# The attention of a graph layer by seven half-size products: a transformer-like kernel on one core

## Chip, cores and metric

The kernel runs on one core of a Trainium2 chip. Its time is the device time of one execution in microseconds. A profile of one execution is shown beside the times; its span is that of the profiled execution alone.

## What is computed

The input x holds 64 graphs of 256 nodes with 512 features, all in fp32, and one adjacency matrix `adj` of 256 x 256 that all graphs share. Two layers follow each other, each with a residual and a layer norm:

```python
def layer0(x, adj, Wq, bq, Wk, bk, Wv, bv, Wo, bo):      # 8 heads of 64
    q, k, v = heads(x @ Wq + bq), heads(x @ Wk + bk), heads(x @ Wv + bv)
    scores = einsum('bqhd,bkhd->bhqk', q, k) / 8 + (1 - adj) * -1e9
    return einsum('bhqk,bkhd->bqhd', softmax(scores), v) @ Wo + bo

def layer1(x, W, a, beta, mask):
    h = x @ W
    e = leaky_relu((h @ a1)[:, :, None] + (h @ a2)[:, None, :], 0.2) * mask
    att = softmax(e, axis=2)
    return elu(att @ h + beta * h)

x1 = layernorm(x + layer0(x, adj, ...))
out = layernorm(x1 + layer1(x1, W, a, beta, adj))
```

In the second layer the kernel doesn't form `h` first. It adds beta to the diagonal of `att`, forms y = (att + beta I) x1 in the "spread" stage, as its transpose `yT`, and then u = y W, to which elu is applied.

## The kernel before

Every tensor is laid out in tiles of 128 partitions. A batch is one graph: x1 is a tile `X` of 128 partitions x 2 token blocks x 512 features; transposed tiles such as `xT`, `qT`, `oT` and `yT` have the features on partitions, in four blocks of 128, and the 256 tokens in the free dimension.

**Projections.** `project` multiplies two operands that are each cut into 2 x 2 quarters by Winograd's form of Strassen's method: seven products of half size in place of eight. Some products need sums of quarters as operands. Those of the weights are made once (`weight_sums`), those of a transposed tile for each batch by four chained subtractions on GpSimd (`token_sums`, 128x256 each), one of which overwrites a quarter in place. On TensorE the products run in the order 1, 5, 2, 6, 3, 4, 7 into three PSUM tiles, `chain`, `cross` and `pair`. Product 6 adds onto `chain` after product 1 has been copied out of it, product 3 onto `cross` after product 5, and product 7 onto `chain` after product 6. `gather` gives the two ways out of PSUM: `copy` on ScalarE and `add` on VectorE. For the projection o, both are an addition to `X` on VectorE. A weight quarter has two blocks of 128 along the contraction, so a product that is laid out by feature (q and k) has 2 x 2 matmuls with 128 columns, and one laid out by token (v, o and u) has 2 with 256 columns.

**Spread.** It is the one large product of the second layer that isn't cut in this way. For each of two groups `g`, four matmuls of 256 columns form half of `yT` in a PSUM tile `ps_y`. The first half is copied out by VectorE (L775), the second by ScalarE (L773). Then `token_sums` makes the sums of `yT` for the projection u.

**Order.** All work is entered into a `Plan` as operations with an engine, an assumed duration, reads, writes and buffers. TensorE's order is written out by hand: an operation carries a turn (round, place in `ROUND`), and a round works on several batches at once. In round R it has the mix and o and logits and attention of batch R-1, the scores, sums and v of batch R, x (the transposes), q and k of batch R+1, and spread and u of batch R-2. Of the last 70 TensorE operations the planner may choose the order itself. For the other engines the planner puts operations in the order in which they can start, those with the earliest due time first among equals. Each engine then takes its instructions in that order. Input and output transfers are issued by SyncE.

**Buffers.** Tiles share slots by tag: "x" 5, "full" 9, "half" 24, "xS" 4 (the sums of tokens), "ps" 8 (PSUM banks). A tile takes its slot with its first operation or with the TensorE operation that claims it ahead.

**Names and lines.** L496 transposes x; L499 copies that to xT; L501 adds the output bias to X. L551 is the mix (attention times V), L617 its scaling into oT; L574 the scores; L581, L583 and L585 are mask, exponential and the sum of both key blocks (`both`) on VectorE, ScalarE and GpSimd; L597 the denominators ("sums"); L601 their reciprocal. L360 is any sum of `token_sums`; L382 and L386 are the matmuls of `project` by feature and by token; L517 and L526 its copies and additions, L700 o's additions. L456 to L466 are a layer norm (`rs` on GpSimd in L460 and L461). L715 makes the logits' dot products (`junk`), L725 transposes them (`tr_s`), L735 is the mask of `e` on GpSimd. L753 transposes the attention (`tr_a`), L757 copies it to `attT`, and L768 is the spread.

Of the kernel before, what the change touches and what calls it, by code (L numbers as in the profile page):

```python
# [12 lines left out]
ALU = mybir.AluOpType  # L13
# [3 lines left out]
P = 128  # L17
# [2 lines left out]
ALPHA = 0.2  # L20
NEG = -1000000000.0

ROUND = ("mix", "scores", "x", "spread", "o", "u", "sums", "v", "logits", "q", "k", "attention")
SAFE = 1e15


# [196 lines left out]
def gnn_two_layers(ctx: ExitStack, tc: tile.TileContext, x, adj, Wq, bq, Wk, bk, Wv, bv, Wo, bo, W, a, beta, out):  # L223
    nc = tc.nc
    B, N, D = x.shape
    NT = N // P
    C = D // P
    H = D // HD
    F = D // 2
# [106 lines left out]
    def weight_sums(w, name, engine, reads=()):  # L336

        S = once([3, 2, F], name)
        eng, ns = (nc.vector, 700) if engine == "DVE" else (nc.gpsimd, 1300)
        w11, w12, w21, w22 = ((lambda c=c, i=i: w[:, 2 * c:2 * c + 2, half(i)]) for i in range(2) for c in range(2))  # L340
        s2, s3, s4 = ((lambda i=i: S[:, i]) for i in range(3))

        plan.op(engine, ns, lambda: eng.tensor_tensor(s3(), w11(), w21(), ALU.subtract), [w] + list(reads), [(S, 3)])
        plan.op(engine, ns, lambda: eng.tensor_tensor(w21(), w21(), w22(), ALU.add), [w, (S, 3)], [(S, 1)])
        plan.op(engine, ns, lambda: eng.tensor_tensor(s2(), w21(), w11(), ALU.subtract), [w, (S, 1)], [(S, 2)])
        plan.op(engine, ns, lambda: eng.tensor_tensor(s4(), w12(), s2(), ALU.subtract), [w, (S, 2)], [(S, 4)])

        return [(w11, w), (w12, w), (s4, (S, 4)), (w22, w), (w21, (S, 1)), (s2, (S, 2)), (s3, (S, 3))]

    def token_sums(T, keys, name):  # L350

        S = sb("xS", [3, 2, P], name)
        q = {(k, j): (lambda k=k, j=j: T[:, 2 * k:2 * k + 2, blk(j)]) for k in range(2) for j in range(2)}
        t2, t3, t4 = ((lambda i=i: S[:, i]) for i in range(3))

        def sub(dst, p, m, reads, writes):
            plan.op("POOL", 725, lambda: nc.gpsimd.tensor_tensor(dst(), p(), m(), ALU.subtract), reads, writes)  # L360

        sub(t3, q[1, 1], q[0, 1], [keys(1, 1), keys(0, 1)], [(S, 1)])
        sub(q[0, 1], q[0, 1], q[0, 0], [keys(0, 1), keys(0, 0)], [keys(0, 1)])
        sub(t2, q[1, 1], q[0, 1], [keys(1, 1), keys(0, 1)], [(S, 0)])
        sub(t4, q[1, 0], t2, [keys(1, 0), (S, 0)], [(S, 2)])
        return [(q[0, 0], [keys(0, 0)]), (q[1, 0], [keys(1, 0)]), (q[1, 1], [keys(1, 1)]), (t4, [(S, 2)]),
                (q[0, 1], [keys(0, 1)]), (t2, [(S, 0)]), (t3, [(S, 1)])]

    def project(left, right, by_feature, claims, copy, add):

        shape = [2, P] if by_feature else [F]
        chain, cross, pair = ps(shape, "ps_chain"), ps(shape, "ps_cross"), ps([2] + shape, "ps_pair")

        def product(n, dst, start):
            l, r = left[n - 1][0](), right[n - 1][0]()
            if by_feature:
                for f in range(2):  # L380
                    for c in range(2):
                        nc.tensor.matmul(dst[:, f, :], l[:, c, blk(f)], r[:, c, :],  # L382
                                         start=start and f == 0 and c == 0, stop=c == 1, skip_group_check=True)
            else:
                for c in range(2):
                    nc.tensor.matmul(dst, r[:, c, :], l[:, c, :], start=start and c == 0, stop=c == 1,  # L386
                                     skip_group_check=True)

        def pe(n, buf, part, start, after=()):
            acc = (lambda: buf[A]) if part is None else (lambda: buf[:, part])  # L390
            key = (buf, part)
            plan.op("PE", 895 if by_feature else 870, lambda: product(n, acc(), start), [left[n - 1][1]] + right[n - 1][1] + list(after), [key], claims=claims)
# [58 lines left out]
    left = {}  # L451
# [18 lines left out]
    def batch(b, at, general=False):  # L470

        X = sb("x", [NT, D], f"x_{b}")
        n = b or 0

        def turn(what):

            later = {"x": -1, "q": -1, "k": -1, "scores": 0, "v": 0, "sums": 0, "mix": 1, "o": 1, "logits": 1,
                     "attention": 1, "spread": 2, "u": 2}[what]
            plan.turn = (n + later, ROUND.index(what if b != 0 or what != "sums" else "logits"))

# [3 lines left out]
        def tokens(t):  # L484
            return [(X, (t, 0)), (X, (t, 1))]
# [18 lines left out]
        if b == 0:  # L504
            plan.turn = (0, ROUND.index("spread"))
            left["o"] = residual_bias()
# [3 lines left out]
        right = token_sums(xT, lambda k, j: (xT, j), "xS")  # L510

        def gather(quarter, bias=None):

            def copy(q, acc):
                (dst, key), (src, acc) = quarter(q), acc[::-1]
                if bias is None:
                    plan.op("ACT", 400, lambda: nc.scalar.copy(dst(), src()), [acc], [key])  # L517
# [229 lines left out]
        tra = ps([NT, N], "tr_a")  # L747
        attT = sb("half", [NT, N], "attT")
# [5 lines left out]

        turn("attention")
        plan.op("PE", 430, pe_att, [e], [tra], claims=[attT])
        plan.op("ACT", 590, lambda: nc.scalar.copy(attT[A], tra[A]), [tra], [attT])  # L757

        yT = sb("full", [C, N], f"yT_{b}")

        def spread(g):
            acc = ps([2, N], "ps_y")

            def pe():
                for i in range(2):
                    c = 2 * g + i
                    for j in range(NT):
                        nc.tensor.matmul(acc[:, i, :], X[:, j, c * P:(c + 1) * P], attT[:, j, :],  # L768
                                         start=j == 0, stop=j == NT - 1)

            plan.op("PE", 1720, pe, tokens(0) + tokens(1) + [attT], [acc], claims=[yT])
            if g:
                plan.op("ACT", 590, lambda: nc.scalar.copy(yT[:, 2 * g:2 * g + 2, :], acc[A]), [acc], [(yT, g)])  # L773
            else:
                plan.op("DVE", 690, lambda: nc.vector.tensor_copy(yT[:, 2 * g:2 * g + 2, :], acc[A]), [acc], [(yT, g)])  # L775

        turn("spread")
        for g in range(2):
            spread(g)
        right_y = token_sums(yT, lambda k, j: (yT, k), "yS")  # L780
        u = sb("full", [NT, D], f"u_{b}")
        turn("u")
        project(left["w"], right_y, False, [u], *gather(
# [3 lines left out]
        for t in range(NT):  # L787
            m = sb("half", [D], "m")
# [12 lines left out]
    for b in range(B):  # L801
        batch(b, slice(b, b + 1))
# [6 lines left out]
    def check():  # L809
# [5 lines left out]
            claims=[least])  # L815
# [9 lines left out]
    with tc.If(again != 0):  # L825
# [40 lines left out]
```

## Time and profile before

| | |
|---|---|
| median of three runs | 2891.65 us (2891.22 to 2893.65) |
| span of the profiled execution | 2892.0 us |
| granted TensorE clock, mean | 0.995 |
| matmuls of the spread (L768) | 1024 records, 236.0 us |
| GpSimd, mean of one L360 | 725 to 738 ns at 128x256 |
| bytes moved by DMA | 110.89 MB, 38 GB/s |

In the profile PE is TensorE's matmul side, PEld its weight loads, DVE VectorE, ACT ScalarE, POOL GpSimd and SP SyncE. An fp32 matmul of the program appears as two records, and the recorded durations of successive matmuls overlap; the cost of a stage is read from the distance between starts. Lines of groups give the operation, out<-in and shapes, how many, busy time, mean duration, and the idle time before them with what ended it. Lines in order of time give start, duration, engine, line and operation, and in brackets the idle time before and its releaser.

### The profile page before, as it was taken

The numbers are of one execution on the slowest core, as the hardware profiler recorded it, in microseconds if no ns is written. First come the engines' busy times: TensorE is split into PE (matmuls) and PEld (weight loads), VectorE is DVE, ScalarE is ACT, GpSimd is POOL, SyncE is SP. The second block draws the span as 40 slices with busy tenths as digits, with TensorE's granted clock in tenths as the row PEclk, the third lists the DMA queues.
The fourth block names the chain that finished last, engine by engine and source line by source line (L and its number), as shares of the span: only waits on it lengthen the run. The fifth ranks groups of instructions, "written<-read, shape, count | busy, mean of one in ns | idle before, by whom it ended". The sixth has DMA issues, their size and how long they took to land.

```text
span 2892.0 us, 51909 instructions
## 1 busy us (share of the span) xinstructions
PE 2852.6 (99%) x19605; PEld 2477.5 (86%) x19605; DVE 1895.8 (66%) x4322; ACT 1293.3 (45%) x3201; POOL 1361.9 (47%) x2010
## 2 busy tenths in 40 slices
PE   8999999999999999999999999999999999999996
PEld 7888888888888888888888888888888888888884
DVE  5666666666666666666666666666666666666666
ACT  3444444444444444444444444444444444444442
POOL 6454453553544544535535445445355354454543
PEclk9999999999999999999999999999999999999998
DMA  3001011011011010111110110111101101111000
GB/s 132 24 30 45 30 38 45 30 38 44 25 44 38 30 45 30 38 45 30 37 45 23 45 37 31 45 30 37 45 30 38 45 23 45 35 33 45 30 23 31
DMA packets 75407, 110.89 MB, mean 38 GB/s; under 512 B 5904, under 2 KB 39440, under 8 KB 75152
## 3 DMA queue, kind: packets, MB, share of 16 engines
q1 hardware_dynamic: 75024, 107.50, 11.3%
q8 instruction: 158, 2.59, 0.4%
q14 instruction: 97, 0.79, 0.1%
q0 software_dynamic: 128, 0.01, 0.0%
HBM read 73.41 MB, written 34.08 MB: 37 GB/s over the span
## 4 chain that ended last, share of the span: by engine, by line
PE 97%; DVE 1%; POOL 1%; issue 0%; DMA 0%; ACT 0%; POOLq 0%; DVEq 0%
PE ps_chain L386 17%; PE ps_chain L382 12%; PE ps_pair L386 11%; PE ps_cross L386 11%; PE ps_cross L382 8%; PE ps_pair L382 8%; PE ps_sc L574 8%; PE ps_pv L551 8%; PE ps_y L768 8%; PE tr_x L496 2%; PE ps_den L597 2%; PE tr_a L753 1%; PE tr_s L725 0%; DVE junk L715 0%; DMA beta_sb<-in_L_gnn_beta_dram 0%
## 5 line engine op out<-in xcount | busy, mean ns | idle before, releaser
L360 POOL TENSOR_TENSOR oS<-oT 128x256 f32<-128x256 f32 x128 | 93.7, 732 | 725.1 <-DVE oT L617 720.0
L583 ACT ACTIVATE pT<-pT 128x512 f32<-128x512 f32 x512 | 297.7, 627 | 303.2 <-DVE pT L581 303.2
L735 POOL TENSOR_TENSOR e<-e,adj_sb 128x512 f32<-128x512 f32 x64 | 81.6, 1275 | 662.4 <-DVE e L733 656.4
L585 POOL TENSOR_TENSOR both<-pT 128x256 f32<-128x256 f32 x512 | 360.9, 734 | 35.8 <-ACT pT L583 35.8
L581 DVE TENSOR_TENSOR pT<-ps_sc,maskT_sb 128x512 f32<-128x512 f32 x512 | 317.4, 682 | 22.8 <-PE ps_sc L574 22.7
L517 ACT COPY u<-ps_chain 128x256 f32<-128x256 f32 x128 | 47.6, 372 | 442.6 <-PE ps_chain L386 442.6
L574 PE MATMUL ps_sc<-qT,kT 64*128 64x256 f32 x2048 | 238.4, 382 | 0.0
L768 PE MATMUL ps_y<-attT,x 128*128 128x256 f32 x1024 | 236.0, 384 | 1.4 <-ACT attT L757 1.4
L551 PE MATMUL ps_pv<-pT,v 128*64 128x256 f32 x2048 | 235.1, 382 | 0.0
L574 PEld LDWEIGHTS ps_sc<-qT,kT 64*128 64x128 f32 x2048 | 192.8, 187 | 43.8 <-issue 24.0
L768 PEld LDWEIGHTS ps_y<-attT,x 128*128 128x128 f32 x1024 | 192.0, 193 | 26.7 <-ACT attT L757 2.2
L551 PEld LDWEIGHTS ps_pv<-pT,v 128*64 128x64 f32 x2048 | 141.4, 137 | 75.5 <-issue 10.3
L466 ACT ACTIVATE x<-x,nmr,rs 128x512 f32<-128x512 f32 x256 | 194.5, 809 | 17.4 <-DVE nmr L464 17.4
L617 DVE TENSOR_TENSOR oT<-ps_pv,inv_all 128x512 f32<-128x512 f32 x128 | 88.5, 692 | 162.2 <-PE ps_pv L551 162.2
L700 DVE TENSOR_TENSOR x<-x,ps_chain 128x256 f32<-128x256 f32 x256 | 102.1, 420 | 138.0 <-PE ps_chain L386 137.2
L715 DVE SCALAR_TENSOR_TENSOR junk<-x,wa_sb 128x512 f32<-128x512 f32 x256 | 165.3, 701 | 0.9 <-ACT x L466 0.9
L501 POOL TENSOR_TENSOR x<-x,res_sb 128x512 f32<-128x512 f32 x128 | 164.4, 1285 | 3.1 <-DVE res_sb L422 3.1
L456 DVE BATCH_NORM_STATS2 bn<-x 128x6 f32<-128x512 f32 x256 | 164.1, 683 | 2.2
L520 ACT ACTIVATE qT<-ps_chain,bq_sb 128x128 f32<-128x128 f32 x256 | 80.3, 365 | 187.9 <-PE ps_chain L382 187.9
L461 POOL TENSOR_TENSOR rs<-rs,neg_half 128x1 f32<-128x1 f32 x256 | 144.2, 563 | 21.3
L382 PE MATMUL ps_chain<-xS,sq_sb 128*128 128x128 f32 x1024 | 135.9, 276 | 0.0
L382 PE MATMUL ps_chain<-xS,sk_sb 128*128 128x128 f32 x1024 | 135.4, 275 | 0.0
(174 smaller groups left out, 6799.0 us busy)
## 6 DMA issues: line engine op xcount, KB each, us to landing
x<-in_x_dram SPq DMA_DIRECT2D x64, 512.0 KB, 3.7
inv_all<-rows SPq DMA_DIRECT2D x128, 256.0 KB, 3.6
out_dram<-x SPq DMA_DIRECT2D x128, 256.0 KB, 2.0
wq_sb<-in_L_gnn_Wq_dram SPq DMA_DIRECT2D x1, 1024.0 KB
wk_sb<-in_L_gnn_Wk_dram SPq DMA_DIRECT2D x1, 1024.0 KB
wo_sb<-in_L_gnn_Wo_dram SPq DMA_DIRECT2D x1, 1024.0 KB
wv_sb<-in_L_gnn_Wv_dram SPq DMA_DIRECT2D x1, 1024.0 KB
w_sb<-in_L_gnn_W_dram SPq DMA_DIRECT2D x1, 1024.0 KB, 14.4
```

What stands on the lines that cost most here:

```text
L382: nc.tensor.matmul(dst[:, f, :], l[:, c, blk(f)], r[:, c, :], start=start and f == 0 and c == 0, stop=c == 1, skip_group_check=True)
L386: nc.tensor.matmul(dst, r[:, c, :], l[:, c, :], start=start and c == 0, stop=c == 1, skip_group_check=True)
L456: plan.op("DVE", 690, lambda: nc.vector.bn_stats(bn[A], X[:, t, :]), [(X, (t, 0)), (X, (t, 1))], [bn])
L466: plan.op("ACT", 810, lambda: nc.scalar.activation(X[:, t, :], X[:, t, :], AF.Identity, bias=nm[A], scale=rs[A]), [nm, rs], [(X, (t, 0)), ...
L501: plan.op("POOL", 1270, lambda: nc.gpsimd.tensor_tensor(X[:, t, :], X[:, t, :], res_sb[A], ALU.add), [res_sb], tokens(t))
L551: nc.tensor.matmul(acc[s * HD:(s + 1) * HD, i, :], V[:, k, h * HD:(h + 1) * HD], pT[h][:, k, :], start=k == 0, stop=k == NT - 1)
L574: nc.tensor.matmul(acc[i + s][:, k, :], kT[r:r + HD, h // 2, blk(k)], qT[r:r + HD, h // 2, :], start=True, stop=True)
L581: plan.op("DVE", 690, lambda h=h, i=i: nc.vector.tensor_add(pT[h][A], acc[i][A], maskT_sb[A]), [acc[i], maskT_sb], [pT[h]])
L583: plan.op("ACT", 620, lambda h=h: nc.scalar.activation(pT[h][A], pT[h][A], AF.Exp, scale=1.0 / HD ** 0.5), [pT[h]], [pT[h]])
L585: plan.op("POOL", 725, lambda h=h: nc.gpsimd.tensor_tensor(both[h // 2][:, h % 2, :], pT[h][:, 0, :], pT[h][:, 1, :], ALU.add), [pT[h]], [ ...
L715: plan.op("DVE", 780, lambda t=t, i=i, junk=junk: nc.vector.scalar_tensor_tensor(junk[A], X[:, t, :], 1.0, wa_sb[:, i, :], op0=ALU.mult, o ...
L768: nc.tensor.matmul(acc[:, i, :], X[:, j, c * P:(c + 1) * P], attT[:, j, :], start=j == 0, stop=j == NT - 1)
```

## The change

The spread is computed by `project` as well. Its left operands are the four quarters of x1 (token block by half of the features) and four sums of them (128x256 each, in a new "full" tile `X_sums`); its right operands are the four 128x128 quarters of the transposed attention, one of them overwritten in place, and three sums (in a new "xS" tile). All eight sums are made on GpSimd. A quarter has one block along the contraction (`inner=1`), so that a product has two matmuls with 128 columns. The four quarters of `yT` come out of PSUM by `gather`: four copies on ScalarE and four additions on VectorE. The two `ps_y` tiles and their two copies are gone. `project` takes a list of dependencies for a left operand too.

In `ROUND`, o follows scores and the spread follows o; x comes after the spread, where it was ahead of it; u moves from behind o to behind the logits, ahead of q.

```diff
-ROUND = ("mix", "scores", "x", "spread", "o", "u", "sums", "v", "logits", "q", "k", "attention")
+ROUND = ("mix", "scores", "o", "spread", "x", "sums", "v", "logits", "u", "q", "k", "attention")
...
-    def project(left, right, by_feature, claims, copy, add):
+    def project(left, right, by_feature, claims, copy, add, inner=2):
...
-                    for c in range(2):
+                    for c in range(inner):
                         nc.tensor.matmul(dst[:, f, :], l[:, c, blk(f)], r[:, c, :],
-                                         start=start and f == 0 and c == 0, stop=c == 1, skip_group_check=True)
+                                         start=start and f == 0 and c == 0, stop=c == inner - 1,
+                                         skip_group_check=True)
...
-        plan.op("ACT", 590, lambda: nc.scalar.copy(attT[A], tra[A]), [tra], [attT])
+        plan.op("ACT", 590, lambda: nc.scalar.copy(attT[A], tra[A]), [tra], [(attT, i) for i in range(4)])
+
         yT = sb("full", [C, N], f"yT_{b}")
-
-        def spread(g):
-            acc = ps([2, N], "ps_y")
-
-            def pe():
-                for i in range(2):
-                    c = 2 * g + i
-                    for j in range(NT):
-                        nc.tensor.matmul(acc[:, i, :], X[:, j, c * P:(c + 1) * P], attT[:, j, :],
-                                         start=j == 0, stop=j == NT - 1)
-
-            plan.op("PE", 1720, pe, tokens(0) + tokens(1) + [attT], [acc], claims=[yT])
-            if g:
-                plan.op("ACT", 590, lambda: nc.scalar.copy(yT[:, 2 * g:2 * g + 2, :], acc[A]), [acc], [(yT, g)])
-            else:
-                plan.op("DVE", 690, lambda: nc.vector.tensor_copy(yT[:, 2 * g:2 * g + 2, :], acc[A]), [acc], [(yT, g)])
-
+        S, T = sb("full", [4, F], "X_sums"), sb("xS", [3, P], "att_sums")
+        x1 = {(i, c): (lambda i=i, c=c: X[:, c, half(i)]) for i in range(2) for c in range(2)}
+        aq = {(c, j): (lambda c=c, j=j: attT[:, c, blk(j)]) for c in range(2) for j in range(2)}
...
+        pool(725, sums[2], x1[0, 0], x1[1, 0], sub, tokens(0), [(S, 3)])
+        pool(725, sums[0], x1[1, 0], x1[1, 1], add, tokens(0) + tokens(1), [(S, 1)])
+        pool(725, sums[1], sums[0], x1[0, 0], sub, tokens(0) + [(S, 1)], [(S, 2)])
+        pool(725, sums[3], x1[0, 1], sums[1], sub, tokens(1) + [(S, 2)], [(S, 4)])
+        pool(450, tsum[1], aq[1, 1], aq[0, 1], sub, [attT], [(T, 1)])
+        pool(450, aq[0, 1], aq[0, 1], aq[0, 0], sub, [(attT, 0), (attT, 1), (attT, 2), (attT, 3), (T, 1)], [(attT, 1)])
+        pool(450, tsum[0], aq[1, 1], aq[0, 1], sub, [(attT, 3), (attT, 1)], [(T, 0)])
+        pool(450, tsum[2], aq[1, 0], tsum[0], sub, [(attT, 2), (T, 0)], [(T, 2)])
...
         turn("spread")
-        for g in range(2):
-            spread(g)
-        right_y = token_sums(yT, lambda k, j: (yT, k), "yS")
+        project(left_x, right_a, True, [yT], *gather(
+            lambda q: (lambda: yT[:, 2 * q[0]:2 * q[0] + 2, blk(q[1])], (yT, q))), inner=1)
+        right_y = token_sums(yT, lambda k, j: (yT, (k, j)), "yS")
```

More of the change, by code (lines that the diff above doesn't have):

```diff
@@ L346, in weight_sums @@
         plan.op(engine, ns, lambda: eng.tensor_tensor(s4(), w12(), s2(), ALU.subtract), [w, (S, 2)], [(S, 4)])
-        return [(w11, w), (w12, w), (s4, (S, 4)), (w22, w), (w21, (S, 1)), (s2, (S, 2)), (s3, (S, 3))]
+        return [(w11, [w]), (w12, [w]), (s4, [(S, 4)]), (w22, [w]), (w21, [(S, 1)]), (s2, [(S, 2)]), (s3, [(S, 3)])]
     def token_sums(T, keys, name):
@@ L391, in pe @@
             key = (buf, part)
-            plan.op("PE", 895 if by_feature else 870, lambda: product(n, acc(), start), [left[n - 1][1]] + right[n - 1][1] + list(after), [key], claims=claims)
+            plan.op("PE", 448 * inner if by_feature else 870, lambda: product(n, acc(), start),
+                    left[n - 1][1] + right[n - 1][1] + list(after), [key], claims=claims)
             return key, acc
@@ new lines, in batch, with pool @@
+        x1 = {(i, c): (lambda i=i, c=c: X[:, c, half(i)]) for i in range(2) for c in range(2)}
+        aq = {(c, j): (lambda c=c, j=j: attT[:, c, blk(j)]) for c in range(2) for j in range(2)}
+        sums = [(lambda i=i: S[:, i]) for i in range(4)]
+        tsum = [(lambda i=i: T[:, i]) for i in range(3)]
+        def pool(ns, dst, p, m, op, reads, writes):
+            plan.op("POOL", ns, lambda: nc.gpsimd.tensor_tensor(dst(), p(), m(), op), reads, writes)
+        sub, add = ALU.subtract, ALU.add
@@ new lines, in batch, with one @@
+        pool(450, tsum[0], aq[1, 1], aq[0, 1], sub, [(attT, 3), (attT, 1)], [(T, 0)])
+        pool(450, tsum[2], aq[1, 0], tsum[0], sub, [(attT, 2), (T, 0)], [(T, 2)])
+        def one(ap):
+            return lambda: ap().unsqueeze(1)
+        s1, s2, s3, s4 = ((one(sums[k]), [(S, k + 1)]) for k in (0, 1, 2, 3))
+        left_x = [(one(x1[0, 0]), tokens(0)), (one(x1[0, 1]), tokens(1)), s4, (one(x1[1, 1]), tokens(1)), s1, s2, s3]
+        right_a = [(one(aq[0, 0]), [(attT, 0)]), (one(aq[1, 0]), [(attT, 2)]), (one(aq[1, 1]), [(attT, 3)]),
+                   (one(tsum[2]), [(T, 2)]), (one(aq[0, 1]), [(attT, 1)]), (one(tsum[0]), [(T, 0)]),
+                   (one(tsum[1]), [(T, 1)])]
```

## The prediction

> **What bounds the kernel now.** I read the page's busy times first, then the busy time by stretch, then the order of time on TensorE, then the groups, and last the other engines' order of time.
>
> ```profile
> PE 2852.6 (99%) x19605; PEld 2477.5 (86%) x19605; DVE 1895.8 (66%) x4322; ACT 1293.3 (45%) x3201; POOL 1361.9 (47%) x2010
> ```
>
> A busy share proves little by itself, as matmul records overlap. The busy time of one round (the columns are PE, PEld, DVE, ACT, POOL, then the granted clock) says more:
>
> ```profile
> 1426.53:1470.76 44.23, 44.23 (x307) 38.52 (x307) 29.24 (x68) 20.15 (x50) 20.91 (x31) 1.00 0.11 37
> ```
>
> PE is never without a matmul at full clock; no other engine is busy over two thirds of the round. 64 rounds of 44.23 us are 2830.7 us of the 2892.0 us span; the other 61 us are head and tail. So a round costs what TensorE must issue, plus any wait that grows past its slack. In order of time on PE (start, us, what):
>
> ```profile
> 1414.39 1.06 PE L382 MATMUL ps_cross<-xT,wq_sb 128*128 128x128 f32 x8
> 1415.28 1.06 PE L382 MATMUL ps_pair<-xT,wq_sb 128*128 128x128 f32 x8
> ...
> 1426.53 3.67 PE L551 MATMUL ps_pv<-pT,v 128*64 128x256 f32 x32
> 1430.14 3.72 PE L574 MATMUL ps_sc<-qT,kT 64*128 64x256 f32 x32
> 1433.79 1.09 PE L496 MATMUL tr_x<-ident,x 128*128 128x128 f32 x8
> 1434.72 3.62 PE L768 MATMUL ps_y<-attT,x 128*128 128x256 f32 x16
> 1438.18 1.03 PE L386 MATMUL ps_chain<-wo_sb,oT 128*128 128x256 f32 x4
> ...
> 1444.22 1.03 PE L386 MATMUL ps_chain<-w_sb,yT 128*128 128x256 f32 x4
> 1445.08 1.03 PE L386 MATMUL ps_cross<-w_sb,yT 128*128 128x256 f32 x4
> ```
>
> Costs are distances of starts. Every written matmul is two records. The spread takes 1438.18 - 1434.72 = 3.46 us for 16 records, 216 ns each at 256 columns. A product of the q projection takes 0.893 us for 8, 112 ns each at 128 columns. Halving the columns halves the cost, weight loads included.
>
> The rest I need is how fast ACT answers PE, and what POOL does:
>
> ```profile
> 1445.34 0.37 ACT L517 COPY u<-ps_chain 128x256 f32<-128x256 f32 x1 [5.85 <-PE ps_chain L386]
> ```
>
> ```profile
> 1431.03 0.72 POOL L360 TENSOR_TENSOR oS<-oT 128x256 f32<-128x256 f32 x1 [11.65 <-DVE oT L617]
> 1431.83 0.73 POOL L360 TENSOR_TENSOR oT<-oT 128x256 f32<-128x256 f32 x1
> ```
>
> ```profile
> 2866.80 0.59 ACT L757 COPY attT<-tr_a 128x512 f32<-128x512 f32 x1 [2.61 <-PE tr_a L753]
> ...
> 2867.43 5.34 PEld L768 LDWEIGHTS ps_y<-attT,x 128*128 128x128 f32 x16 [1.08 <-ACT attT L757]
> ```
>
> A copy starts 0.26 us after its product's last issue slot (1445.08 to 1445.34), takes 0.37 us, and PE goes on 0.04 us after ACT ends (2867.39 to 2867.43). POOL's dependent sums follow each other every 0.81 us, and POOL stands idle 11.65 us before oS in every round.
>
> [...] the trace has 0.893/4 = 223 ns per written matmul. [...] (8 loads hide in each 0.893 us). [...] four L715 operations beside POOL took up to 1.74 us instead of 0.69.
>
> **The change part by part.**
>
> *Spread on PE.* Removed: 8 matmuls of 256 columns, 3.46 us. Added: 7 products of 2 matmuls of 128 columns, 28 records x 111.65 ns = 3.126 us. Gain 0.334 us a round, 64 x 0.334 = 21.4 us. Loads rise from 16 to 28, but in the q ratio of one load to 112 ns, where they are hidden.
>
> *Copies out of PSUM.* ACT loses one 0.586 us copy and gets four of 0.37: +0.9, 21.0 us a round. DVE loses 0.69 and gets four adds of 0.42: +1.0, 30.2 us. Neither fills 43.9 us. But `chain` and `cross` are reused inside the project, and its products are now 0.447 us long. Product 6 may write `chain` only after the copy that follows product 1. Two products, 0.893 us, lie between; the loop is 0.26 + 0.37 + 0.04 = 0.67. Slack 0.22 us, or 0.11 if the load, one 0.11 us slot ahead, must also keep its place. The same holds for 5 to 3 and 6 to 7. If ACT is free, it costs nothing; bound 0 to 0.11 us each.
>
> *Sums on POOL.* Four of 128x256 at 0.81: 3.2 us. The 128x128 size is in no row; 732 and 1275 ns at 256 and 512 elements give 0.46 us, with the 0.08 us step 0.54; at worst as dear as 256, 0.81. Four are 2.2 us (to 3.2). POOL rises from 20.9 to 26.3 of 43.9 us. The attention sums start when attT lands, 0.76 us after the mix begins, and end by 3.0; oS queues behind them and is ready only at 4.5. The spread needs them from 13.8. The sums of x1 have from about 19 us of one round to 13.3 of the next. Hidden, by the projections' matmuls.
>
> *The order.* From the old durations, with 0 at the mix: scores 3.6, o 7.3, spread 13.3, x 16.4, sums 17.4, v 18.5, logits 24.6, u 24.8, q 30.8, k 37.0, attention 43.3, end 43.9. What now comes due earlier:
> - o at 7.3 instead of 11.65. Its product 1 waits for POOL's second sum (it overwrites a part of oT), ready at 4.5 + 2 x 0.81 = 6.1. Slack 1.2. DVE must put o's adds before some pT adds; the first has 1.7 us to be done in, against 0.26 + 0.42 + 0.04 and one pT add of 0.68.
> - sums at 17.4 instead of 23.8. POOL ends oS at 7.7, then eight `both` at 0.70: 13.3. Slack 4. Even one x + res (1.29) in between fits.
> - logits at 24.6. From the end of o (1444.22) to the end of the last junk (1453.33) is 9.1 us now; 13.3 + 9.1 = 22.4. Slack 2.2.
> - u at 24.8: yT is added up by 17.5, yS takes 3.2 us, x + res and rs 4.1: done by 24.8; its first POOL result is needed at 25.6. The end of logits to attention grows from 12.7 to 18.7 us, so nothing there.
> The x load on SP moves 9 us later with its transposes, 13 us ahead of q. The output DMAs follow u and go 7 us later; nothing but the x slots waits for them.
>
> *Buffers.* "full" gets a ninth tile per batch for nine slots. X_sums lives about 40 us; at the worst I count xT, qT, kT, V, inv_all, oT or u, X_sums and yT partly overlapping, seven or eight. xS peaks at three of four. PSUM: o's first bank is the first score bank, free at 5.4.
>
> *Head and tail.* PE waited 4.3 us before the first tr_s; x now lies between o and it, so up to 0.9 less. In the tail the last spread waits for POOL's 2.2 us beside its first two products: about 1 us more. The free reordering window of 70 PE entries covers fewer rounds. I take 0, bounds -3 and +4 us.
>
> Sum: -21.4 + 0 against the 2892.0 us span. The three runs lie at 2891.22 to 2893.65 around 2891.65, from which I subtract: 2870.3.
>
> **The rivals.**
>
> *A: ACT's queue stops the short spread.* ACT takes its instructions in the order that the planner wrote; an exponential of 627 ns (L583) or a norm's 809 ns (L466) in front of the copy of `chain` makes PE late by 0.627 - 0.11 = 0.52 or 0.70 us. It decides from 0.334 us a round: one such meeting a round makes it slower, by 64 x (0.52 - 0.334) = 12 to 64 x 0.37 = 23 us: 2903 to 2915. For it: the last exponential ends 13.0 us after the mix now, and the spread begins at 13.3. Against it: the pT adds of DVE lose the yT copy from their midst, ACT loses two xT copies there, and norm x1 follows o's end by 5.6 us, after the spread. But o's adds now lie among the pT adds.
>
> *B: small stalls eat part of it.* POOL at `both` or yS, DVE at o's adds, or the tight copy loop at 0.1 us each: 0.1 to 0.25 us a round, 2876.7 to 2886.
>
> *C: it isn't less work for PE.* If 28 loads bound at their recorded 192 ns, the spread would take 5.4 us and the kernel 124 us more. The q products exclude it.
>
> **How the numbers follow.** A measurement of this kernel can tell about 0.2%, 5.8 us, from no change. No new wait, 2866 to 2875: 0.63. B with a visible gain: 0.14. Gains and stalls within 0.2% of each other: 0.08. Slower, A with what is left of C: 0.15. So faster 0.77, same 0.08, slower 0.15. The range takes the first case with the end bounds, and B: 2864 to 2889.
>
> **What would show it.** Right: rounds of 43.89 us, PE gapless; the spread 3.13 us from its first product to tr_x; POOL near 26 us a round. The chain copies in the spread start 0.26 us after their product. Wrong: idle PE or PEld in front of a spread product put down to ACT's yT (A), or in front of o, ps_den, tr_s or u (B); or a spread over 3.3 us with no wait.

## The result and the profile after

The changed kernel takes 2875.74 us, the median of four runs (2874.54 to 2876.21); the kernel before takes 2892.19 us, the median of four (2891.22 to 2893.65). The ratio is 0.9942, with an interval of 0.9925 to 0.9959: 16.5 us faster. The forecast was 21.4 us faster. The two profiled spans are 2892.0 and 2874.1 us, 17.9 us apart.

The busy times of the page:

```profile
PE 2838.8 (99%) x20373; PEld 2489.0 (87%) x20373; DVE 2072.5 (72%) x4514; ACT 1385.9 (48%) x3393; POOL 1757.7 (61%) x2522
```

One steady round (the columns are PE, PEld, DVE, ACT, POOL, granted clock, DMA share, GB/s):

```profile
1415.28:1459.35 44.07, 44.07 (x319) 38.71 (x318) 32.11 (x71) 21.63 (x53) 27.10 (x39) 1.00 0.11 37
```

A round lasts 44.07 us where it lasted 44.23 and 43.89 was forecast. POOL carries about what was forecast (26.3), DVE 1.9 us more than its 30.2, and PE is still the engine without a gap. The round, in order of time on PE (start, us):

```profile
1418.89 3.72 PE L576 MATMUL ps_sc<-qT,kT 64*128 64x256 f32 x32
1422.54 1.13 PE L387 MATMUL ps_chain<-wo_sb,oT 128*128 128x256 f32 x4
1423.51 1.03 PE L387 MATMUL ps_cross<-wo_sb,oT 128*128 128x256 f32 x4
...
1428.69 0.61 PE L382 MATMUL ps_chain<-attT,x 128*128 128x128 f32 x4
1429.13 0.61 PE L382 MATMUL ps_cross<-attT,X_sums 128*128 128x128 f32 x4
1429.58 0.61 PE L382 MATMUL ps_pair<-attT,x 128*128 128x128 f32 x4
1430.03 0.61 PE L382 MATMUL ps_chain<-att_sums,X_sums 128*128 128x128 f32 x4
...
1431.81 1.04 PE L498 MATMUL tr_x<-ident,x 128*128 128x128 f32 x8
1432.78 1.07 PE L599 MATMUL ps_den<-both,ones 128*32 128x256 f32 x16
...
1439.93 0.51 PE L727 MATMUL tr_s<-ident,s 128*128 128x128 f32 x2
1440.27 1.03 PE L387 MATMUL ps_chain<-w_sb,yT 128*128 128x256 f32 x4
```

The spread takes 1431.81 - 1428.69 = 3.12 us, a product every 0.445 to 0.45 us with no stall. But the two `tr_s` take 0.34 us up to u's first product, where they took 0.22, and o's first product takes 0.97 where its next takes 0.86. The weight loads show why `tr_s` is late:

```profile
1439.71 0.14 PEld L727 LDWEIGHTS tr_s<-ident,s 128*128 128x128 f32 x1
1440.11 0.13 PEld L727 LDWEIGHTS tr_s<-ident,s 128*128 128x128 f32 x1 [0.26 <-DVE junk L717]
```

The second of them waits for the last logit product on DVE. The view of waits has this for the whole kernel (total us, times, longest us); it counts the idle time of the weight loads, of which PE loses 0.12 us a round:

```profile
PEld tr_s L727 <- DVE junk L717: 22.9, 65, 2.5
```

Before, the same wait came four times. What DVE does up to that product in the kernel before (the last of the four logit products, then the reciprocal), and what POOL did last:

```profile
1452.64 0.69 DVE L715 SCALAR_TENSOR_TENSOR junk<-x,wa_sb 128x512 f32<-128x512 f32 x1
...
1453.25 1.75 DVE L601 RECIPROCAL inv<-ps_den 128x256 f32<-128x256 f32 x1
```

```profile
1460.67 1.28 POOL L735 TENSOR_TENSOR e<-e,adj_sb 128x512 f32<-128x512 f32 x1 [10.64 <-DVE e L733]
```

There POOL stands idle for 10.64 us, beside all four products. DVE in the kernel after:

```profile
1433.94 1.76 DVE L603 RECIPROCAL inv<-ps_den 128x256 f32<-128x256 f32 x1 [0.18 <-PE ps_den L599]
1435.62 1.03 DVE L717 SCALAR_TENSOR_TENSOR junk<-x,wa_sb 128x512 f32<-128x512 f32 x1
...
1438.84 1.21 DVE L717 SCALAR_TENSOR_TENSOR junk<-x,wa_sb 128x512 f32<-128x512 f32 x1
1439.98 0.08 DVE L717 DVE_READ_ACCUMULATOR junk<-x,wa_sb 128x1 f32 x1
```

and POOL at the same time:

```profile
1437.31 1.05 POOL L360 TENSOR_TENSOR xT<-xT 128x256 f32<-128x256 f32 x1
...
1439.58 1.06 POOL L360 TENSOR_TENSOR xS<-xT,xS 128x256 f32<-128x256 f32 x1
```

The reciprocal now stands ahead of the logit products; before it stood behind them. And the products share their time with POOL's sums of `xT`: they take up to 1.21 us instead of 0.69, the sums 1.06 instead of 0.73; these are DVE's 1.9 us. The last product ends at 1440.06, 11.37 us after the end of o (1428.69), where it was 9.1 us before.

Where the 17.9 us of span come from: the second mix starts at 93.42 us instead of 99.81, which is 6.4 us (both read from the chain of work that ended last, which puts a mix 0.07 us later than the order of time does). The 60 rounds from there bring 60 x 0.16 = 9.7. The rest, the tail above all, is 138.6 us before and 136.8 after: 1.8.

### The profile page after: what moved, and what is told of

It reads as the page before. It is cut to its first block, busy times and chain, and to the rows that moved or that the text cites. A ratio compares the mean times of both kernels' runs of the same rounds, so it can differ in the third digit from the quotient of the medians.

```text
span 2874.1 us, 54166 instructions
## 1 busy us (share of the span) xinstructions
PE 2838.8 (99%) x20373; PEld 2489.0 (87%) x20373; DVE 2072.5 (72%) x4514; ACT 1385.9 (48%) x3393; POOL 1757.7 (61%) x2522
## 4 chain that ended last, share of the span: by engine, by line
PE 98%; DVE 1%; POOL 0%; issue 0%; DMA 0%; ACT 0%; POOLq 0%; DVEq 0%
PE ps_chain L387 18%; PE ps_chain L382 15%; PE ps_pair L387 11%; PE ps_cross L387 11%; PE ps_cross L382 10%; PE ps_pair L382 10%; PE ps_sc L576 8%; PE ps_pv L553 8%; PE ps_den L599 2%; PE tr_x L498 2%; PE tr_a L755 1%; PE tr_s L727 1%; DVE junk L717 0%; DMA beta_sb<-in_L_gnn_beta_dram 0%; PE ps_b L420 0%
## 5 line engine op out<-in xcount | busy, mean ns | idle before, releaser
L585 ACT ACTIVATE pT<-pT 128x512 f32<-128x512 f32 x512 | 312.1, 630 | 448.0 <-DVE pT L583 444.3
L462 POOL TENSOR_SCALAR rs<-mv 128x1 f32<-128x1 f32 x256 | 55.9, 219 | 504.3 <-DVE mv L459 504.3
L717 DVE SCALAR_TENSOR_TENSOR junk<-x,wa_sb 128x512 f32<-128x512 f32 x256 | 282.3, 1154 | 0.4 <-ACT x L468 0.3
L770 POOL TENSOR_TENSOR att_sums<-attT 128x128 f32<-128x128 f32 x128 | 58.8, 459 | 323.6 <-ACT attT L759 318.6
L468 ACT ACTIVATE x<-x,nmr,rs 128x512 f32<-128x512 f32 x256 | 200.7, 808 | 72.1 <-DVE nmr L466 63.6
L463 POOL TENSOR_TENSOR rs<-rs,neg_half 128x1 f32<-128x1 f32 x256 | 144.7, 565 | 21.4
L360 POOL TENSOR_TENSOR xS<-xT 128x256 f32<-128x256 f32 x128 | 140.8, 1100 | 8.1 <-ACT xT L501 3.1
L387 PE MATMUL ps_chain<-so_sb,oS 128*128 128x256 f32 x512 | 131.5, 379 | 0.0
L387 PE MATMUL ps_chain<-sw_sb,yS 128*128 128x256 f32 x512 | 131.5, 379 | 0.0
```

The source lines that it names most:

```text
L468: plan.op("ACT", 810, lambda: nc.scalar.activation(X[:, t, :], X[:, t, :], AF.Identity, bias=nm[A], scale=rs[A]), [nm, rs], [(X, (t, 0)), ...
L585: plan.op("ACT", 620, lambda h=h: nc.scalar.activation(pT[h][A], pT[h][A], AF.Exp, scale=1.0 / HD ** 0.5), [pT[h]], [pT[h]])
L717: plan.op("DVE", 780, lambda t=t, i=i, junk=junk: nc.vector.scalar_tensor_tensor(junk[A], X[:, t, :], 1.0, wa_sb[:, i, :], op0=ALU.mult, o ...
```

## The experiments

The theory at first: the products bring their 0.33 us a round, and the new order takes half of it back at its seams and at `tr_s`; the 6.4 us of the head belong to the order as well. The rival: the shorter spread itself is what stalls, or it makes the next stages late. Each experiment changes one thing. This table has the stages of one steady round on PE as distances of starts, in us, for those that differ (mix 3.60, scores 3.65, sums 1.00, q and k 6.25 each and attention 0.53 are the same in all):

| kernel | round | x | o | spread | v | logits | u | second mix starts |
|---|---|---|---|---|---|---|---|---|
| before | 44.23 | 0.93 | 6.04 | 3.46 | 6.15 | 0.22 | 6.14 | 99.81 |
| after | 44.07 | 0.97 | 6.15 | 3.12 | 6.15 | 0.34 | 6.05 | 93.42 |
| order only | 44.27 | 0.97 | 6.15 | 3.45 | 6.15 | 0.22 | 6.05 | 93.59 |
| products only | 43.92 | 0.93 | 6.05 | 3.15 | 6.15 | 0.22 | 6.14 | 98.14 |
| logits behind u | 44.16 | 0.96 | 6.15 | 3.19 | 6.30 | 0.22 | 6.04 | 92.17 |
| x ahead of o | 44.77 | 0.93 | 6.36 | 3.22 | 6.15 | 0.78 | 6.05 | 97.70 |
| new order in round 1 alone | 43.92 | as products only | | | | | | 93.41 |
| reciprocal behind the junks | 43.94 | 0.97 | 6.15 | 3.12 | 6.15 | 0.22 | 6.05 | 93.54 |
| GpSimd held | 43.95 | 0.97 | 6.15 | 3.12 | 6.15 | 0.22 | 6.05 | 92.25 |

**The order alone.** The kernel before with the new `ROUND`, and nothing else:

```diff
-ROUND = ("mix", "scores", "x", "spread", "o", "u", "sums", "v", "logits", "q", "k", "attention")
+ROUND = ("mix", "scores", "o", "spread", "x", "sums", "v", "logits", "u", "q", "k", "attention")
```

> The kernel before with the new order of a round alone; the spread stays one product of 256 columns. Theory 1 (boundaries): the round pays for the order what the changed kernel shows against 44.23 us: +0.11 us where o instead of x follows the scores, +0.04 for the transposes ahead of the denominators, -0.09 for u no longer ahead of them; 44.29 us if the logits don't wait, 44.41 if they do. Theory 2: the order is free and it is the short products that cost 0.18 us a round more than worked out: 44.23 us here. Of the head, theory 1 says that the 6.4 us gained up to the second mix come from the order (o and its norm start earlier): the second mix starts near 93.5 us; if they come from the products, near 99.8. Total by theory 1: -3 to +5 us against the kernel before.

It took 2890.75 us, the kernel before in the same runs 2892.72; the ratio is 0.9993 (0.9985 to 1.0002), not told from no change. Its head has the whole gain (second mix at 93.59) and its rounds lose 0.04 us each: o costs 0.10 more behind the scores, x 0.04 more ahead of the sums, u 0.09 less. `tr_s` doesn't wait: the last junk ends at 1446.54, 11.44 us after the end of o, and `tr_s` comes at 1446.67. It is just met. So the path to the logits is as long here as in the kernel after; the longer spread hides it.

**The products alone.** The kernel after with the old `ROUND`.

```diff
-ROUND = ("mix", "scores", "o", "spread", "x", "sums", "v", "logits", "u", "q", "k", "attention")
+ROUND = ("mix", "scores", "x", "spread", "o", "u", "sums", "v", "logits", "q", "k", "attention")
```

> The changed kernel with the old order of a round. Theory 1: the products bring their whole 0.334 us: rounds of 43.89 us, the second mix near 99.8 us as before, 2871 to 2873 us in all, so 3 to 5 us less than the changed kernel. Theory 2 (short products cost more than worked out, or need the other order since u comes 6 us after the spread): rounds of 44.0 us or more with idle PE in front of a spread product or of u, 2878 us or more.

2873.29 us, ratio 0.9933 (0.992 to 0.9947). The rounds are 0.31 us shorter, and the head gains 1.7 us only. The logit products are stretched here too: beside the new sums of x1 on POOL three of the four take 1.20 us, and the last ends 11.22 us after o, where it was 9.1. In this order that is still 2.06 us ahead of `tr_s`. Here, with the spread close behind the exponentials, ScalarE does what rival A feared. In order of time:

```profile
1425.61 0.63 ACT L585 ACTIVATE pT<-pT 128x512 f32<-128x512 f32 x1
1426.23 0.37 ACT L519 COPY yT<-ps_chain 128x256 f32<-128x256 f32 x1
1426.50 0.64 ACT L585 ACTIVATE pT<-pT 128x512 f32<-128x512 f32 x1
```

and PE beside it:

```profile
1426.03 0.61 PE L382 MATMUL ps_cross<-attT,X_sums 128*128 128x128 f32 x4
1426.48 0.63 PE L382 MATMUL ps_pair<-att_sums,x 128*128 128x128 f32 x4
1426.95 0.61 PE L382 MATMUL ps_chain<-att_sums,X_sums 128*128 128x128 f32 x4
```

Exponentials lie between the copies, yet only one distance is longer, 0.47 instead of 0.45. The copy of product 6 starts 0.20 us after its product's last issue slot (1426.03), as early as a free ScalarE would start it, since the exponential ahead of it ends just then; it is done at 1426.60, 0.35 us ahead of product 7. The exponentials are where rival A puts them, and the spread is 0.02 us longer than in the kernel after. The longer distance is that of product 4, which writes the second half of `pair`: its weight load waits for DVE's addition out of the first half, which ended at 1426.28, and starts at 1426.40, 0.03 us later than the others' distance would have it.

**Logits behind u.** If the wait of `tr_s` is the loss, a later place takes it away:

```diff
+ROUND = ("mix", "scores", "o", "spread", "x", "sums", "v", "u", "logits", "q", "k", "attention")
```

> The changed kernel with u ahead of the logits. Theory 1: the second tr_s transpose waits 0.12 us a round for the last dot product of the logits, which GpSimd's sums beside it stretch from 0.69 to 1.20 us; with 6 us more there is no wait, and the round is 43.95 us, 7 us less in all: 2868 to 2870 us. The dot products stay near 1.2 us. Rival: the attention now gets its inputs too late (logits to attention are back at 12.7 us, with more work on DVE and GpSimd), tr_a waits, and the round is 44.07 us or more.

2878.37 us, ratio 0.9953 (0.9939 to 0.9967): this expectation was missed. `tr_s` is back at 0.22, but v now takes 6.30 us. ScalarE, in order of time:

```profile
1437.41 0.39 ACT L606 ACTIVATE junk<-ps_den 128x256 f32<-128x256 f32 x1 [1.44 <-DVE inv L603]
...
1437.78 0.36 ACT L519 COPY v<-ps_chain 128x256 f32<-128x256 f32 x1
```

The activation of L606 reads the PSUM tile that the reciprocal on DVE also reads, and waits until that is done. v's copy stands behind it in ScalarE's queue, v's next product on `chain` waits for the copy: products at 1437.28, 1438.20 and 1439.17, distances of 0.92 and 0.97 instead of 0.86. The spread took 0.06 more: its sixth product, product 4 again, came 0.06 us late behind an addition of `yT` on DVE (ended 1432.44, load of the product at 1432.49). That is read from one trace and wasn't tested.

**x ahead of o.** Only x's place goes back, and u behind the logits stays; x is then no seam behind the spread:

```diff
+ROUND = ("mix", "scores", "x", "o", "spread", "sums", "v", "logits", "u", "q", "k", "attention")
```

> The changed kernel with x right behind the scores again (logits still ahead of u). Theory 1: the first product after the scores pays for its first weight load: o's start costs 0.11 us, that of the transposes 0.04; GpSimd can make the sums of xT earlier, so the dot products of the logits meet less of it and tr_s falls from 0.34 to 0.22 us: 43.87 to 43.95 us a round, 2864 to 2869 us. Rival (tr_s at 0.34 us is the price of going from a transpose to a product of 256 columns, not a wait): tr_s stays at 0.34 and the round is near 44.0 us, 2871 us. Second rival: x and its sums of xT crowd out the sums for the spread or both, and PE waits: over 44.07 us.

2923.19 us, ratio 1.0105 (1.0089 to 1.012): 30 us slower, where a gain was expected. The wait of `tr_s` grows to 0.78 - 0.22 = 0.56 us, as x no longer lies between o and the logits. o is 0.31 us longer: in a steady round the load of its product 4 starts at 1408.86, as DVE's addition out of the first half of `pair` ended only at 1408.74, behind two mask additions (1.28 us). That is one of the places of rival B, o's adds; it is read from the trace and wasn't tested. The spread's 0.1 us lies in its last distance, ahead of the sums (0.54 instead of 0.445), where u pays the same in the old order. That the wait grows when the time from the end of o to the logits shrinks fits the theory; the late product and the seam were left out of the expectation. The head has little of its gain (97.7), as x is ahead of o in the first round too.

**The new order in round 1 alone.** If the head's 6.4 us come from the order of the first round, they can be had without the 0.15 us that the order costs in each later one:

```diff
-            plan.turn = (n + later, ROUND.index(what if b != 0 or what != "sums" else "logits"))
+            order = EARLY if n + later == 1 else ROUND
+            plan.turn = (n + later, order.index(what if b != 0 or what != "sums" else "logits"))
```

`EARLY` is the new order and `ROUND` the old one.

> The seven products with the old order of a round, but in round 1 alone the new order (o right behind the scores, x after it). Theory: the head of the kernel gains 4.7 us on the products with the old order (second mix at 93.4 instead of 98.1 us), as o of the first batch starts earlier and the first tr_s no longer leaves TensorE idle so long that its clock drops; the rounds stay at 43.92 us: 2873.3 - 4.7 = 2868.6 us. Rival: the time is only moved (round 2 or the tail gives it back): 2873 us.

2867.19 us against 2892.03 of before: ratio 0.9914 (0.9901 to 0.9928), below both kernels. The rounds are those of the products alone, the second mix starts at 93.41. What happens in the head, in the kernel before:

```profile
83.70 0.48 PE L725 MATMUL tr_s<-ident,s 128*128 128x128 f32 x1 [1.96 <-DVE junk L715]
83.97 1.92 PE L382 MATMUL ps_chain<-xT,wq_sb 128*128 128x128 f32 x8
85.68 1.91 PE L382 MATMUL ps_cross<-xT,wq_sb 128*128 128x128 f32 x8
```

and after:

```profile
80.15 0.32 PE L727 MATMUL tr_s<-ident,s 128*128 128x128 f32 x1 [1.52 <-DVE junk L717]
80.31 1.06 PE L382 MATMUL ps_chain<-xT,wq_sb 128*128 128x128 f32 x8
81.20 1.06 PE L382 MATMUL ps_cross<-xT,wq_sb 128*128 128x128 f32 x8
```

The logits are ready 3.55 us sooner (80.15 for 83.70). With x behind it and fewer late products, o ends at 70.25 instead of 71.79 (1.54 us); the first junk starts 5.70 us after that instead of 6.27 (0.57); and the four junks take 4.15 us instead of 5.59 (1.44), as POOL's operations of 512 elements, x + res and a sum of the weights, beside which three of them took 1.62 to 1.74, are elsewhere (three take 1.20 now, beside sums of 256 columns). The q products then start every 0.89 us instead of every 1.71, at a granted clock of 1.00 from the start of q to the mix. The busy time by stretch of the kernel before has 0.50 in its clock column after the wait:

```profile
83.90:89.00 5.10, 5.10 (x25) 5.10 (x25) 1.89 (x5) 1.25 (x4) 1.27 (x1) 0.50 0.00 0
```

From the start of q to the mix it is 15.77 us before and 13.04 after, 2.73 less. Together with 3.55, and 0.11 less at `tr_s`, that is the 6.4. The slow products stand behind the longer idle times: 2.32 + 1.96 = 4.28 us of idle PE before, with one short transpose between, were followed by 5.1 us at 0.50; behind the 1.5 us after, and the 2.06 us in the kernel with the order alone, the products start every 0.89 us from the first on. With the products alone, behind 1.76 + 1.94 = 3.70 us, the first three q products take 1.34, 1.71 and 1.26 us and the next ones 0.89, so that q to the mix takes 14.67 us there; 1.1 of the 1.7 us that its head gains are this. How long the products stay slow was read from one profile of each kernel, and from what idle time on they are slow wasn't shown.

**The reciprocal behind the junks.** In the kernel after, one more read for the reciprocal, `s` of the batch whose logits are due:

```diff
-                plan.op("DVE", 1750, lambda: nc.vector.reciprocal(inv[A], acc[A]), [acc], [inv])
+                plan.op("DVE", 1750, lambda: nc.vector.reciprocal(inv[A], acc[A]), [acc] + dots.get(n - 1, []), [inv])
...
+            dots[n] = s
```

> The changed kernel, in which the planner is told that the reciprocal of the denominators (L603, 1.76 us on VectorE) comes after the dot products of the logits (L717), as it did in the kernel before. Theory: the 0.12 us a round that tr_s waits come from VectorE's queue; with the reciprocal behind, the last dot product ends at least 0.5 us earlier, tr_s takes 0.22 us, and the round is 43.95 us: 7 us less than the changed kernel, 2868 to 2869 us. Rival: ScalarE's sum of the reciprocal's input (L606) waits for the reciprocal, and behind it stand the copies of v, so that v's products wait instead: 44.05 us a round or more.

2870.49 us, ratio 0.9927 (0.9914 to 0.9941). `tr_s` takes 0.22 again and the round 43.94, although the junks still take 1.20 to 1.26 us each. The first of them starts 5.88 us after the end of o instead of 6.93, and the last ends 0.7 us ahead of `tr_s`:

```profile
1434.51 1.20 DVE L718 SCALAR_TENSOR_TENSOR junk<-x,wa_sb 128x512 f32<-128x512 f32 x1
...
1435.65 1.75 DVE L604 RECIPROCAL inv<-ps_den 128x256 f32<-128x256 f32 x1
```

**GpSimd's sums of x behind the junks.** The other half of the path: the sums of `xT`, beside which a junk takes up to 1.21 us instead of 0.69, wait for the junks of batch n-2.

```diff
-        sub(t3, q[1, 1], q[0, 1], [keys(1, 1), keys(0, 1)], [(S, 1)])
+        sub(t3, q[1, 1], q[0, 1], [keys(1, 1), keys(0, 1)] + list(later), [(S, 1)])
...
+        right = token_sums(xT, lambda k, j: (xT, j), "xS", dots.get(n - 2, []))
```

> The changed kernel, in which the planner is told that GpSimd's sums of xT come after the dot products of the logits. Theory: [...] without that three dot products are 0.5 us shorter each, the last ends 1.5 us earlier, and tr_s doesn't wait: 43.95 us a round, 2868 to 2870 us, L717 near 0.7 us. Rival: some other GpSimd sum (of x1 or of yT) moves into the same place, L717 stays near 1.2 us and tr_s waits as before: 44.07 us, 2875.7 us.

2874.11 us, ratio 0.9939 (0.9925 to 0.9952), rounds of 44.06: no change. The rival held. The sums of x1 (`X_sums`) moved into the free place on POOL, and the junks still took about 1.2 us.

**GpSimd quiet, in the plan.** The sums of x1 are sent behind the junks too (`+ s` in the reads of the first two of them).

> The changed kernel, in which the planner is told that GpSimd's sums of xT and those of x1 both come after the dot products of the logits, so that GpSimd has nothing but the rest of the sums of yT to do beside them; the reciprocal stays ahead of them. Theory: GpSimd's sums are what stretches L717; it falls from 1.20 to about 0.69 us, the last dot product ends 1.5 us earlier, tr_s takes 0.22 instead of 0.34 us, and the round is 43.95 us: 2868 to 2871 us. Rival: L717 is stretched by something else (ScalarE, DMA, its own operands) and stays near 1.2 us: tr_s waits as before, 44.07 us a round, 2875 us. Third: the delayed sums come too late for q (xS) and PE waits there: over 44.1 us.

2910.64 us, ratio 1.0062 (1.0048 to 1.0076): not met, as the planner now put the residual's x + res, 512 elements wide, on POOL beside a junk. DVE and POOL:

```profile
1452.79 1.75 DVE L718 SCALAR_TENSOR_TENSOR junk<-x,wa_sb 128x512 f32<-128x512 f32 x1
```

```profile
1452.27 1.72 POOL L504 TENSOR_TENSOR x<-x,res_sb 128x512 f32<-128x512 f32 x1
```

A junk took 1.75 us, `tr_s` 0.88 and the round 44.60. That fits the theory from the other side, but the run didn't take POOL's work away.

**GpSimd held.** POOL gets an instruction of its own, a sum of two dot products (128x2), which can't run before the junks; the sums of `xT`, of x1 and x + res read its result.

```diff
+        hold = st(2, "hold")
+        if not general:
+            plan.op("POOL", 200, lambda: nc.gpsimd.tensor_tensor(hold[A], s[0][A], s[1][A], ALU.add), s, [hold])
+            dots[n] = [hold]
```

> As the run before, but GpSimd is really held: a sum of the two 128x2 results of the dot products (0.2 us on GpSimd) stands in its queue ahead of the sums of xT, of those of x1 and of the bias added to x, so that none of them can start beside L717. Theory: without GpSimd beside it L717 takes 0.69 us, its last one ends over a microsecond before tr_s needs it, tr_s takes 0.22 us and the round is 43.95 us: 2868 to 2871 us. Rival: L717 is stretched by something else: it stays at 1.2 us or more, and tr_s at 0.34 us or more. Third: GpSimd's work, put off by 3 us, makes q or the next mix wait: L717 at 0.69 us, tr_s at 0.22, but idle PE elsewhere and over 44.07 us a round.

2869.18 us against 2892.18: ratio 0.992 (0.9907 to 0.9934). POOL, DVE and PE:

```profile
1430.55 0.72 POOL L360 TENSOR_TENSOR yS<-yT,yS 128x256 f32<-128x256 f32 x1
1433.75 0.19 POOL L726 TENSOR_TENSOR hold<-s 128x2 f32<-128x2 f32 x1 [2.47 <-DVE junk L718]
```

```profile
1432.98 0.68 DVE L718 SCALAR_TENSOR_TENSOR junk<-x,wa_sb 128x512 f32<-128x512 f32 x1
```

```profile
1435.12 0.38 PE L732 MATMUL tr_s<-ident,s 128*128 128x128 f32 x2
```

With POOL idle for 2.47 us the junk takes 0.68 (the first of the four, still beside a sum of `yT`, takes 1.02), the last one ends at 1433.68, 1.4 us ahead of `tr_s`, and the round is 43.95. The reciprocal stays ahead of the junks here (1429.13 to 1430.89). So either half, taken away, is enough.

**One copy twice.** The forecast had 0.22 us of slack in the loop over `chain`, less if the weight load must keep its place. To measure it, a spare copy of the same PSUM tile (into a tile that nothing else uses) goes ahead of the copy of product 1 and of that of product 6:

```diff
+                    if q in twice:
+                        spare = sb("half", [2, P], "spare")
+                        plan.op("ACT", 400, lambda: nc.scalar.copy(spare[A], src()), [acc], [spare])
+                        first = [spare]
+                    plan.op("ACT", 400, lambda: nc.scalar.copy(dst(), src()), [acc] + first, [key])
```

> The changed kernel with the two copies of the spread's chain made twice (once into a spare tile ahead of the real one), to measure how much slack the short products leave ScalarE. By the prediction's loop (0.2 to 0.26 us to start, now 2 x 0.37 us of copies, 0.04 us back, against 0.893 us with the weight load 0.11 us ahead) product 6 and product 7 are each 0.1 to 0.25 us late, and product 3 follows a late copy of cross too: the round grows by 0.2 to 0.6 us, 13 to 38 us in all. If the short products are not bound by these copies at all, the time stays at 2875 us.

2892.11 us, ratio 0.9999 (0.999 to 1.0008). ScalarE, PE and the weight loads:

```profile
1435.33 0.37 ACT L522 COPY spare<-ps_chain 128x256 f32<-128x256 f32 x1 [1.41 <-PE ps_chain L382]
1435.60 0.38 ACT L524 COPY yT<-ps_chain 128x256 f32<-128x256 f32 x1
```

```profile
1435.52 0.61 PE L382 MATMUL ps_pair<-attT,x 128*128 128x128 f32 x4
1436.03 0.71 PE L382 MATMUL ps_chain<-att_sums,X_sums 128*128 128x128 f32 x4
1436.58 0.61 PE L382 MATMUL ps_cross<-attT,X_sums 128*128 128x128 f32 x4
```

```profile
1435.41 0.53 PEld L382 LDWEIGHTS ps_pair<-attT,x 128*128 128x128 f32 x4
1436.03 0.52 PEld L382 LDWEIGHTS ps_chain<-att_sums,X_sums 128*128 128x128 f32 x4
```

The real copy ends 0.91 us after its product's last issue slot (1435.07 to 1435.98) instead of 0.57: 0.27 for the spare copy, and 0.06 as the first of the two starts at 0.26 instead of 0.20, for which no cause was found. In the kernel after, the load of product 6 starts 0.11 us ahead of its matmul (1429.92 and 1430.03); here the copy holds it back until 1436.03, 0.62 us after the load before it instead of 0.445, so 0.17 late. PE loses the same: its distances are 0.51 and 0.55 instead of 0.445 each, 0.17 in all. The same happens at product 7. The spread is 3.45 us, +0.33; `tr_s` then no longer waits (0.22), and the round is 0.21 us longer than in the kernel after, 12 us in all. The other 4.8 of the 17.1 us of span lie behind the steady rounds, so that the total meets the expectation (13 us or more) only with them.

## Why the forecast was right in sign and 5 us too large

**The spread's 0.334 us on PE: right.** 3.12 us after, 3.126 forecast; the products alone bring 0.31 a round. Rival C, that 28 loads bind, is excluded: the distances stay at 0.445.

**The copies out of PSUM: right.** The copy that gates product 6 starts 0.20 us after its product's last issue slot (0.26 forecast):

```profile
1429.33 0.37 ACT L519 COPY yT<-ps_chain 128x256 f32<-128x256 f32 x1 [1.35 <-PE ps_chain L382]
```

With 0.37 and 0.05 the loop is 0.62 of 0.893. Of the forecast's two figures for the slack the second holds, in which the load must keep its place: 0.893 - 0.62 - 0.11 = 0.16 us (0.11 forecast, with the later start). The doubled copy ended 0.34 us later and made the load 0.17 late, so the slack was 0.17. Rival A's exponentials between the copies occur with the old order, and there they make no product late, where 0.52 to 0.70 us were feared: it supposed an exponential that starts just before the copy is due, and in the round shown it ends there.

**The sums on POOL: right.** 128x128 takes 0.46 us at steps of 0.53 (0.54 forecast):

```profile
1416.11 0.46 POOL L770 TENSOR_TENSOR att_sums<-attT 128x128 f32<-128x128 f32 x1 [5.00 <-ACT attT L759]
1416.64 0.46 POOL L770 TENSOR_TENSOR attT<-attT 128x128 f32<-128x128 f32 x1
```

All four are done at 1418.17, 10.5 us ahead of the spread, and in the steady rounds nothing on PE waits for POOL.

**"Logits at 24.6 ... Slack 2.2": the step that failed.** It carried the 9.1 us from the end of o to the end of the last junk over from the old order, as if that were a duration. It is a queue. The first junk starts 6.93 us after o instead of 6.59: three additions of u are gone from the time ahead of it (1.3 us), and four of `yT` and the reciprocal (1.76) have come in; without the reciprocal it starts at 5.88. The four junks take 4.44 us instead of 2.52, beside POOL's sums. 9.1 + 0.34 + 1.92 = 11.37 us, where the stages between leave 3.12 + 0.97 + 1.00 + 6.15 = 11.24. The slack of 2.2 became a wait of 0.12 us. The prediction had half of the cause in hand: it quoted L715 at up to 1.74 us beside POOL in the head (three of the four there, the fourth took 0.68), and didn't ask which POOL work the new sums and the new order lay beside the junks. `tr_s` stands among the signs that it gave for rival B, but its slack there was taken for safe. Two runs show it: moving the reciprocal and holding POOL each bring `tr_s` back to 0.22 and the round to 43.94 or 43.95.

**The order at no cost: wrong by 0.04 us.** Shown by the order alone: o's first product costs 0.10 more behind the scores, x 0.04 more, u 0.09 less. For o, the trace has the first weight load only as its matmul starts, not ahead of it:

```profile
1422.54 0.73 PEld L387 LDWEIGHTS ps_chain<-wo_sb,oT 128*128 128x128 f32 x4 [0.33 <-DVE pT L583]
```

Before, o followed the spread, and u the o. Now o (128 x 128 in the view) follows matmuls of another tile, the scores (64 x 128), as v's first product follows the denominators (128 x 32) and costs the same 0.97. That the change of tile keeps the load back is the author's guess and wasn't shown; no run separates it from a wait.

**Head and tail at 0, bounds -3 and +4: wrong.** The head gave 6.4 us, 3.55 of it sooner logits and 2.7 the clock. The prediction saw the 4.3 us wait and allowed up to 0.9 for x; it missed that o then ends sooner, that the stretched junks it had quoted lose part of the POOL work beside them, and above all that the 5.1 us behind that wait ran at a granted clock of 0.50. The tail's spread does wait for `attT`, but the part behind the steady rounds is 1.8 us shorter, not 1 longer. What makes that up stays open; in the other kernels this part lasts from 135 to 142 us, so edits that don't aim at it move it by more than that.

**The sum.** Forecast a round: -0.334. Measured: -0.31 for the products in the old order, +0.04 for the order, +0.12 for `tr_s`, which comes only where both meet: -0.14 to -0.15. The measured difference is 0.16; the 0.02 left over are the spread's, 3.12 us behind o and 3.15 in the old order. Over the 60 steady rounds that is 9.7 us instead of 20; the head brings 6.4 and the end 1.8 that weren't forecast. That the total came within 5 us of the forecast is in part luck: half of the gain in the rounds was lost, and most of the loss was made up where none was expected. The result falls between the forecast's first case and rival B, which had the size of the stalls (0.1 to 0.25 us a round, 0.17 measured) but named POOL at `both` or yS, o's adds or the copies as their place.

## What to carry to other kernels

When a stage is moved, don't carry a distance such as "end of o to last junk" to the new place: write out each engine's queue in between again, with what the new order puts ahead of the work and what it lays beside it on engines that slow it, as the logit products took up to 1.21 us instead of 0.69 beside POOL's sums here. A slack of 2 us in a round of 44 was gone through one reciprocal and four stretched operations, and taking away either was enough to be rid of the wait. And where a new order helps in the first round only, use it there only: that version is the fastest here, 2867.19 us.

## What the hardware showed that was not expected

A logit product of 128x512 on VectorE took 0.68 us alone, 1.20 beside sums of 256 columns on GpSimd and 1.75 beside one of 512; the GpSimd side took 1.06 instead of 0.73, and 1.72. A product whose weight load was held back by 0.17 us, until a copy out of PSUM was done, cost PE 0.17 us, though the order of time shows its own matmul only 0.06 us late. An activation that reads a PSUM tile which VectorE is reading waited 1.44 us for the end of that read, and the copy behind it cost PE 0.16 us a round; the trace puts the end of the wait down to a semaphore that the reciprocal updates, so it is an order that the program carries; whether the two reads could run side by side wasn't tried.
